# Graph attention on one core: gathers without memsets between them, and a rearranged end of each layer

## The chip, the cores and the metric

The kernel runs on one core of one Trainium2 chip. The metric is the device time of one execution in microseconds (us); the median of several executions is compared. The engines are named as in the profile: PE is TensorE's matmul, PEld its weight load, DVE is VectorE, ACT is ScalarE, POOL is GpSimd, SP is SyncE. The letter q behind a name means the engine's queue (waits, register work, issuing of transfers).

## The reference

A graph of 6250 nodes with 256 features and 200,000 edges (src, dst, 32 edge features), the edges sorted by dst. Two graph-attention layers, the first with 4 heads, the second with 1:

```python
h = relu(layernorm(x))
# per layer:
te  = relu(edge_attr @ We + be) * exp(x @ Wo + bo)[src][:, None]
hx  = (x @ Wg).reshape(n, heads, f)
al  = leaky_relu((hx*a_s).sum(-1)[src] + (hx*a_d).sum(-1)[dst] + ((te @ Wge)*a_e).sum(-1), 0.2)   # self loops added
al  = exp(al - segment_max(al, dst)[dst]);  al = al / segment_sum(al, dst)[dst]
out = segment_sum(hx[src] * al, dst) + b
# layer 0: x = relu(out + x);  layer 1: x = out + x + h;  result = input x + that
```

All arithmetic that matters here is float32.

## The kernel before

**Tables.** A prologue computes one row per node, `hx` with the node's attention terms, into a table in device memory (`T[0]`, 268 numbers a row). Layer 0 writes the rows of layer 1 into a second table (`T[1]`); each of its rows is twice 260 numbers wide, a table row and a kept input, so that layer 1 addresses it with twice the node's number.

**Steps.** The edges lie in chunks of 128, one edge per partition and chunk; a superchunk is up to 24 chunks. There are 66 superchunks to a layer: 64 of 24 chunks, then one of 14 and one of 13. `edges` walks over 132 steps, 0 to 65 for layer 0 and 66 to 131 for layer 1. A step has a dictionary `st`: its tile `G` (gathered rows), `S` (one-hot matrix by destination), `rt` and `ade` (edge and destination terms), `U` (sums by destination).

**Order.** Nothing is scheduled by a planner: the order of each engine's queue is the order in which the Python code issues (`manual_schedule`). Waits between engines are put in by the framework from the parts of tiles that instructions read and write. In `edges`, the iteration of step `st` also prepares the next step `nx`:

- POOL: `gather(nx)` issues one indirect transfer for each chunk (line 799): 128 rows, picked by a column of `self.src`, land in one chunk of `G`. Three tiles for `G` are used in turn, so the gathers of step k wait for the sums of step k-3. Behind each gather stands a memset of a tile `gap` of 208 numbers per partition (line 803); nothing reads `gap`. The rows of step 0 are gathered from `x` in the prologue (line 249), without memsets.
- DVE: `logits(st)` (lines 987 to 1002), the first to read all of `G`; `spread`, `parts`, `blocks` for `nx`; `links(st)` (1020, 1022), `maxima(st)` (1037 to 1064), `scale(st)` (1095), `carried(st)` (1077 to 1085), `edge_rows(nx)` (973, 976), `onehots(nx)` (927, 930), and `finish(pv)` for the nodes of the step before.
- PE: `ends(st)` (1010, a transpose that `links` needs), `rphase1` and `rphase2` (885, 899) and `adst` (959) for `nx`, the transpose in `links` (1027), then `sums(st)` (1105): one matmul `u += S^T G` per chunk. `rows1`, `rows2` (1198, 430) make the rows of layer 1 for finished nodes.
- ACT: the activations of `rphase1` (890), the exponentials (1060, 1135, 1147), `evict` (1110, `u` to `U`). SP: the other transfers, among them the store of a finished group of nodes in `rows3` (1239 in layer 0, 1244 in layer 1).

**A layer's end.** `ending(st, nx, pv, late, after)` replaces the loop's body where `st` is the superchunk of 14 chunks and `nx` that of 13. `pv` and `late` are earlier steps whose nodes are unfinished; `after` is the first step of the next layer, or None. In it `finish(pv, Z)` and `finish(st, Z)` do the wide part of layer 0's node update on POOL (`Z = nc.gpsimd`). `sums(nx, first=1)` takes chunk 0 last, since the sums carried over from the step before are added to that chunk. Line 750 doubles all of `self.src` at once, for layer 1's addresses. In layer 1, the nodes of the last two superchunks are stored by an indirect transfer on POOL (1249), and not on SP.

Of the kernel before, what the change touches and what calls it, by code (L numbers as in the profile page):

```python
# [22 lines left out]
F32 = mybir.dt.float32  # L23
BF = mybir.dt.bfloat16
I32 = mybir.dt.int32
AF = mybir.ActivationFunctionType
OP = mybir.AluOpType
# [4 lines left out]
P = 128  # L32
C = 24
# [46 lines left out]
class Kernel:  # L80
# [322 lines left out]
    def fixed_rows(self):  # L403
        nc, cp = self.nc, self.cp
        self.crow = cp.tile([1, D + self.L[0].H], F32, name="crow")
        self.cl = [cp.tile([36, P + 1], F32, name=f"cl{i}") for i in range(2)]
        for t in self.cl:
            nc.gpsimd.memset(t, -BIG)

        self.cnt = cp.tile([P, self.NS, 2], F32, name="cnt")  # L410
        self.mt = cp.tile([P, 4 * C + 4], F32, name="mt")
        self.gap = cp.tile([P, 208], F32, name="gap")
        self.fb = [cp.tile([P, 37 * C], F32, name=f"fb{i}") for i in range(2)]
        for t in [self.mt] + self.fb:
            nc.gpsimd.memset(t, 0.0)


        self.aq = [cp.tile([P, 4, 32], BF, name=f"aq{i}") for i in range(2)]
        for t in self.aq:
            nc.gpsimd.memset(t, 0.0)  # L420
        self.trow1 = []
        L1 = self.L[1]
        for i in range(2):
            self.trow1.append(cp.tile([P, 2 * L1.TW], F32, name=f"t1row{i}"))
            nc.gpsimd.memset(self.trow1[i][:, L1.TW + D:], 0.0)
# [135 lines left out]
    def index_group(self, g, pool, di):  # L561
# [23 lines left out]
        for pen, e in zip((self.fpen, self.lpen), ends):  # L585
            t = pool.tile([P, 4 * C], F32, name="gt", bufs=2)
            e3 = e.to_broadcast([P, n, c])
            V.tensor_sub(v3(t[:, :w]), *((d3, e3) if pen is self.fpen else (e3, d3)))
            yield
            V.tensor_scalar(pen[:, o:o + w], t[:, :w], 1.0, -BIG, op0=OP.min, op1=OP.mult)  # L590
            yield
# [117 lines left out]
    def ending(self, st, nx, pv, late, after):  # L709

        nc, k = self.nc, st["k"]
        Z = nc.gpsimd
        self.load_lb(k + 3)
        self.gather(nx)
        drain(self.logits(st))
        self.ends(st)
        self.spread(nx)
        self.parts(nx)
        y = self.rphase1(nx)
        next(y)  # L720
        self.links(st)
        if late:
            self.rows2(late)
        self.blocks(nx)
        drain(y)
        self.load_ea(k + 2)
        self.rphase2(nx)
        self.adst(nx)
        drain(self.maxima(st))
        drain(self.scale(st))  # L730
        self.carried(st)
        self.sums(st)
        self.edge_rows(nx)
        drain(self.logits(nx))
        self.ends(nx)
        self.onehots(nx)
        if late:
            self.rows3(late)
        if pv:
            drain(self.finish(pv, Z))  # L740
        self.links(nx)
        self.load_fl(k + 2)
        drain(self.maxima(nx))
        self.evict(st)
        y = self.rphase1(after) if after else iter(())
        next(y, None)
        c = nx["C"]
        drain(self.scale(nx, cuts=(1, 1 + c // 2, c)))
        if after:
            nc.vector.tensor_scalar(self.src, self.src, 2.0, None, op0=OP.mult)  # L750
        drain(self.scale(nx, cuts=(0, 1)))
        self.carried(nx)
        self.sums(nx, first=1)
        self.evict(nx)
        drain(self.finish(st, Z))
        if pv:
            self.rows1(pv)
            self.rows2(pv)
            self.rows3(pv)
        drain(y)  # L760
        f = self.finish(nx)
        while after and "hw" not in nx:
            next(f)
        self.rows1(st)
        self.rows2(st)
        drain(f)
        self.rows3(st)
        self.rows1(nx)
        self.rows2(nx)
        self.rows3(nx)  # L770
        if after:
            self.gather(after)
            self.nodes(after)
            self.spread(after)
            self.parts(after)
            self.blocks(after)
            self.rphase2(after)
            self.adst(after)
            self.edge_rows(after)
            self.onehots(after)  # L780
# [11 lines left out]
    def gather(self, st):  # L792
        nc, L = self.nc, st["L"]
        st["G"] = G = self.G0 if st["k"] == 0 else self.gp[st["k"] % 3].tile([P, C, 270], F32, name="G")
        n = self.N
        idx = self.src[:, st["o"]:st["o"] + st["C"]]
        last = st["C"] - 1
        for c in (range(0) if st["k"] == 0 and self.CX > last else (last, *range(last))):
            nc.gpsimd.indirect_dma_start(  # L799
                out=G[:, c, 0:L.TW], out_offset=None, in_=self.rows[L.l][0:n * (1 + L.l), :],  # L800
                in_offset=bass.IndirectOffsetOnAxis(ap=idx[:, c:c + 1], axis=0))
            if st["k"]:
                nc.gpsimd.memset(self.gap, 0.0)  # L803

    def pair(self, k):

# [198 lines left out]

    def ends(self, st):


        e = st["ends"]
        self.nc.tensor.transpose(self.lf[0:e.shape[1], 1:P + 1], e, self.ident)  # L1010
# [85 lines left out]
                                    .to_broadcast([P, c1 - c0, H, L.F]), op=OP.mult)  # L1096
            yield

    def sums(self, st, first=0):
        nc, L, c = self.nc, st["L"], st["C"]  # L1100
        G, S = st["G"], st["S"]
        st["u"] = self.ps_1.tile([P, 512], F32, name="u")
        for j in range(c):
            i = (j + first) % c
            nc.tensor.matmul(st["u"][:, :L.W], S[:, i, :], G[:, i, 0:L.W], start=(j == 0), stop=(j == c - 1))  # L1105

    def evict(self, st):
        L = st["L"]
# [125 lines left out]
    def rows3(self, st):  # L1234
        nc, L, s = self.nc, st["L"], st["s"]
        if L.l == 0:
            self.table_row(st)
            r = self.row(0, s)
            nc.sync.dma_start(self.T[1][ds(r, M), :], st["trow"][1:M + 1, :])
            return  # L1240
        o, out = st["o"], self.a["out"]
        if s < self.direct:
            r = self.row(1, s)
            nc.sync.dma_start(out[ds(r, M), :], o[1:M + 1, :])
        else:
            idx = self.np_.tile([P, 1], I32, name="oidx")
            nc.vector.tensor_add(idx, self.base_f[:, s:s + 1], self.iota_m)
            nc.vector.memset(idx[0:1, :], 1 << 20)
            nc.gpsimd.indirect_dma_start(  # L1249
                out=out[:, :], out_offset=bass.IndirectOffsetOnAxis(ap=idx[:, 0:1], axis=0), in_=o,  # L1250
                in_offset=None, bounds_check=self.N - 1, oob_is_err=False)
# [119 lines left out]
def drain(g):  # L1371
    for _ in g:
        pass
# [93 lines left out]
```

## Time and profile before

| | |
|---|---|
| runs | 4551.79, 4556.36, 4559.2 us (median 4556.36) |
| profiled execution | 4555.93 us, span of its instructions 4554.1 us |
| busy | PE 3065.9 us (67%), PEld 1899.5 (42%), DVE 2901.8 (64%), ACT 516.8 (11%), POOL 3915.8 (86%) |
| gathers of line 799 | 3102, 2969.6 us busy |
| memsets of line 803 | 3102, 893.3 us busy |
| granted TensorE clock | 0.743 of full speed on average |

Busy time is what an engine's instructions took. In a list of groups, behind the bar stand the busy time in us, the mean of one instruction in ns, and the idle time of the engine just before such instructions with what ended it. A timeline row is: start in us, duration in us, engine, line, operation, output <- input, count, and in brackets the engine's idle time before it and what released it. The POOL span of a gather is the work of issuing it; when its data have landed is told in a row of its own ("DMA to landing").

### The profile page before, as it was taken

To read this page: it belongs to the slowest core of one execution; us is meant where nothing else is said; L and a number is where in the kernel's file an instruction comes from. 1 tells how busy PE (TensorE), PEld (TensorE's weight loads), DVE (VectorE), ACT (ScalarE), POOL (GpSimd) and SP (SyncE) were. 2 spreads that over 40 slices of the span, in tenths; PEclk is the share of its full clock that TensorE was granted. 3 is DMA by queue.
4 is the path that set the end of the run, shared out by engine and by line. 5 is a ranking of instruction groups with operands and counts; after the bars stand their busy time and mean duration, and the time that the engine had idled before them with its cause. 6 is when DMAs were issued, how large, how long until landed. Compare 5 with 4: busy or idle time off the path is not lost. (4 is left out here: it accounts for less than half of the span.)

```text
span 4554.1 us, 37613 instructions
## 1 busy us (share of the span) xinstructions
PE 3065.9 (67%) x9916; PEld 1899.5 (42%) x9916; DVE 2901.8 (64%) x6675; ACT 516.8 (11%) x1150; POOL 3915.8 (86%) x6365
## 2 busy tenths in 40 slices
PE   8777677667677677677746566666666665666665
PEld 6444444444444344444424334333343343433433
DVE  7877667677677677676745555555554555555655
ACT  5111111111111111111100000000000000000000
POOL 6888888888888888888878888888888888888885
PEclk9877777777777777777767777777777777777777
DMA  6444444444444444444434444444444444444442
GB/s 224 130 136 134 126 129 136 124 127 136 125 128 135 125 128 135 125 130 134 119 98 124 116 128 122 118 128 128 111 128 121 124 123 128 122 116 122 128 116 74
DMA packets 231112, 576.39 MB, mean 127 GB/s; under 512 B 63097, under 2 KB 87871, under 8 KB 230825
## 3 DMA queue, kind: packets, MB, share of 16 engines
q0 software_dynamic: 150144, 422.75, 35.2%
q1 hardware_dynamic: 80331, 150.52, 10.0%
q8 instruction: 79, 1.29, 0.1%
q14 instruction: 142, 1.16, 0.1%
q10 hardware_dynamic: 416, 0.67, 0.1%
HBM read 542.72 MB, written 31.09 MB: 126 GB/s over the span
## 5 line engine op out<-in xcount | busy, mean ns | idle before, releaser
L799 POOL DMA_INDIRECT G<-T,src x3102 | 2969.6, 957 | 553.1 <-issue 518.7
L1105 PE MATMUL u<-G,S 128*128 128x270 f32 (+1 forms) x6252 | 1461.0, 393 | 106.7 <-DVE G L1085 97.6
L1105 PEld LDWEIGHTS u<-G,S 128*128 128x128 f32 x6252 | 1189.5, 192 | 388.0 <-DVE G L1085 162.1
L803 POOL MEMSET gap<- 128x208 f32 x3102 | 893.3, 288 | 1.8
L1095 DVE TENSOR_TENSOR G<-G,kps 128x6144 f32<-128x6144 f32 (+3 forms) x136 | 853.0, 6274 | 0.0
L885 PE MATMUL y<-ea,webd 64*128 64x384 f32 (+1 forms) x1056 | 749.7, 860 | 67.3 <-ACT R L890 66.7
L1010 PE MATMUL lf<-ident,fb 128*36 128x128 f32 (+1 forms) x132 | 53.3, 404 | 1093.3 <-DVE fb L1002 772.3
L987 DVE TENSOR_TENSOR G<-rt,G 128x96 f32<-128x96 f32 (+1 forms) x132 | 30.2, 228 | 1138.9 <-DMA G<-T,src 1138.6
L1010 PEld LDWEIGHTS lf<-ident,fb 128*36 128x36 f32 (+1 forms) x132 | 15.7, 119 | 1134.6 <-DVE fb L1002 819.2
L899 PE MATMUL zad<-R,wea 128*64 128x384 f32 (+1 forms) x1056 | 476.0, 815 | 0.5 <-DVE aq L952 0.3
L890 ACT ACTIVATE R<-y,webd 128x768 f32<-128x768 f32 x260 | 233.2, 897 | 2015.2 <-PE lf L1027 1647.7
L930 DVE TENSOR_TENSOR S<-kps,loc 128x3072 f32<-128x3072 f32 x132 | 437.5, 3315 | 4.5
L885 PEld LDWEIGHTS y<-ea,webd 64*128 64x128 f32 x1056 | 300.9, 314 | 311.8 <-issue 192.5
L899 PEld LDWEIGHTS zad<-R,wea 128*64 128x64 f32 x1056 | 160.7, 207 | 319.0 <-issue 214.0
L945 PE MATMUL zad<-a,Q 128*128 128x12 bf16 (+1 forms) x132 | 24.9, 188 | 174.6 <-DVE a L943 174.6
L430 PE MATMUL fin<-wg,h1T 128*128 128x260 f32 x264 | 135.3, 667 | 2.3 <-ACT h1T L1200 2.3
L973 DVE STREAM_TRANSPOSE rt<-zad 128x768 f32<-128x768 f32 (+1 forms) x130 | 124.9, 960 | 12.1 <-PE zad L959 11.2
L914 DVE TENSOR_TENSOR lb<-lb,kps 128x1536 bf16<-128x1536 bf16 (+1 forms) x68 | 112.7, 1658 | 0.0
L1110 ACT ACTIVATE U<-u 128x270 f32<-128x270 f32 (+1 forms) x132 | 51.9, 393 | 493.7 <-PE u L1105 493.7
L1041 DVE SCALAR_TENSOR_TENSOR m<-fpen,lf,m 128x24 f32<-128x24 bf16 (+1 forms) x66 | 16.4, 249 | 132.8 <-PE lf L1027 132.6
L945 PEld LDWEIGHTS <-Q 128*128 128x128 bf16 x132 | 13.7, 104 | 208.3 <-DVE a L943 198.6
L430 PEld LDWEIGHTS fin<-wg,h1T 128*128 128x128 f32 x264 | 75.6, 316 | 52.1 <-issue 36.6
(201 smaller groups left out, 2287.5 us busy)
## 6 DMA issues: line engine op xcount, KB each, us to landing
G<-T,src POOLq DMA_INDIRECT x3102, 2.8
ea<-in_ea_dram SPq DMA_DIRECT2D x64, 768.0 KB
lb<-locrow SPq DMA_DIRECT2D x64, 384.0 KB
T<-t1row SPq DMA_DIRECT2D x66, 227.5 KB
tw<-T SPq DMA_DIRECT2D x66, 225.8 KB
tw<-T SPq DMA_DIRECT2D x66, 117.2 KB
tw<-in_x_dram SPq DMA_DIRECT2D x66, 112.0 KB
out_dram<-fb SPq DMA_DIRECT2D x64, 112.0 KB
```

Of the source, the lines that this page charges most:

```text
L430: self.nc.tensor.matmul(ps[:, :L.MW], hT[:, k, :], self.wg[L.l][:, k, :], start=(k == 0), stop=(k == 1))
L799: nc.gpsimd.indirect_dma_start(out=G[:, c, 0:L.TW], out_offset=None, in_=self.rows[L.l][0:n * (1 + L.l), :], in_offset=bass.IndirectOffset ...
L803: nc.gpsimd.memset(self.gap, 0.0)
L885: nc.tensor.matmul(y[:, o], self.webd[l][r, :], ea[r, w], start=True, stop=True)
L890: nc.scalar.activation(R[:, i, :32 * c].rearrange("p (b n) -> p b n", b=2), y.rearrange("p (b n) -> p b n", b=2)[:, :, :16 * c], AF.Relu, ...
L899: nc.tensor.matmul(st["zad"][i * PH:(i + 1) * PH, o], self.wea[l][0], R[:, i, w], start=True, stop=False)
L914: V.tensor_tensor(lb[:, :, :n], lb[:, :, :n], self.k_part.unsqueeze(2).to_broadcast([P, i, n]), op=OP.is_equal)
L930: nc.vector.tensor_tensor(st["S"][:, c0:c1, :], self.k_iota.unsqueeze(1).to_broadcast(w), self.loc[:, o + c0:o + c1].unsqueeze(2).to_broad ...
L973: V.transpose(rv[:, :32 * c].rearrange("p (b n) -> p b n", b=2), z.rearrange("p (b n) -> p b n", b=2)[:, :, :16 * c])
L1010: self.nc.tensor.transpose(self.lf[0:e.shape[1], 1:P + 1], e, self.ident)
L1095: nc.vector.tensor_tensor(v, v, pw[:, c0:c1, :].unsqueeze(3) .to_broadcast([P, c1 - c0, H, L.F]), op=OP.mult)
L1105: nc.tensor.matmul(st["u"][:, :L.W], S[:, i, :], G[:, i, 0:L.W], start=(j == 0), stop=(j == c - 1))
```

## The change

1. `gather` no longer puts a memset behind each transfer, and the tile `gap` is gone.
2. `ends` doubles the step's own columns of `self.src` in layer 0; the doubling of all columns in `ending` is gone.
3. In `ending`, `sums(st)` is issued in three parts (4, 4 and 6 of 14 chunks): before `edge_rows(nx)`, behind `ends(nx)`, and behind `links(nx)`. `finish(pv)` and `finish(st)` run on DVE. `links(nx)` comes ahead of `rows3(late)` and `finish(pv)`; `evict(nx)` comes behind a part or all of `finish(st)`; the rows of finished nodes move accordingly.
4. The index of the indirect stores at the end of layer 1 is computed at the start of `ending`.

```diff
@@ fixed_rows
-        self.gap = cp.tile([P, 208], F32, name="gap")
@@ ending
-        Z = nc.gpsimd
         self.load_lb(k + 3)
         self.gather(nx)
+        for q in () if after else (st, nx):
+            q["idx"] = idx = self.np_.tile([P, 1], I32, name="oidx")
+            nc.vector.tensor_add(idx, self.base_f[:, q["s"]:q["s"] + 1], self.iota_m)
+            nc.vector.memset(idx[0:1, :], 1 << 20)
         drain(self.logits(st))
         self.ends(st)
...
         self.carried(st)
-        self.sums(st)
+        c, h = nx["C"], st["C"] // 3
+        self.sums(st, (0, h))
         self.edge_rows(nx)
         drain(self.logits(nx))
         self.ends(nx)
+        self.sums(st, (h, 2 * h))
         self.onehots(nx)
-        if late:
-            self.rows3(late)
-        if pv:
-            drain(self.finish(pv, Z))
         self.links(nx)
+        self.sums(st, (2 * h, st["C"]))
         self.load_fl(k + 2)
         drain(self.maxima(nx))
         self.evict(st)
         y = self.rphase1(after) if after else iter(())
         next(y, None)
-        c = nx["C"]
         drain(self.scale(nx, cuts=(1, 1 + c // 2, c)))
-        if after:
-            nc.vector.tensor_scalar(self.src, self.src, 2.0, None, op0=OP.mult)
         drain(self.scale(nx, cuts=(0, 1)))
         self.carried(nx)
-        self.sums(nx, first=1)
-        self.evict(nx)
-        drain(self.finish(st, Z))
+        self.sums(nx, (1, c), (0, 1))
+        if late:
+            self.rows3(late)
         if pv:
+            drain(self.finish(pv))
             self.rows1(pv)
             self.rows2(pv)
+            if not after:
+                self.rows3(pv)
+        f = self.finish(st)
+        while after and "hw" not in st:
+            next(f)
+        if not after:
+            drain(f)
+            self.rows3(st)
+        self.evict(nx)
+        drain(f)
+        if after and pv:
             self.rows3(pv)
         drain(y)
+        self.rows1(st)
+        self.rows2(st)
         f = self.finish(nx)
         while after and "hw" not in nx:
             next(f)
-        self.rows1(st)
-        self.rows2(st)
+        if after:
+            self.rows3(st)
         drain(f)
-        self.rows3(st)
         self.rows1(nx)
@@ gather
-            if st["k"]:
-                nc.gpsimd.memset(self.gap, 0.0)
@@ ends
+        if st["L"].l == 0:
+            src = self.src[:, st["o"]:st["o"] + st["C"]]
+            self.nc.vector.tensor_scalar(src, src, 2.0, None, op0=OP.mult)
@@ sums
-    def sums(self, st, first=0):
+    def sums(self, st, *parts):
...
-        st["u"] = self.ps_1.tile([P, 512], F32, name="u")
-        for j in range(c):
-            i = (j + first) % c
-            nc.tensor.matmul(st["u"][:, :L.W], S[:, i, :], G[:, i, 0:L.W], start=(j == 0), stop=(j == c - 1))
+        for a, b in parts or ((0, c),):
+            for i in range(a, b):
+                j = st["n"] = st.get("n", -1) + 1
+                if j == 0:
+                    st["u"] = self.ps_1.tile([P, 512], F32, name="u")
+                nc.tensor.matmul(st["u"][:, :L.W], S[:, i, :], G[:, i, 0:L.W], start=(j == 0), stop=(j == c - 1))
@@ rows3
-            idx = self.np_.tile([P, 1], I32, name="oidx")
-            nc.vector.tensor_add(idx, self.base_f[:, s:s + 1], self.iota_m)
-            nc.vector.memset(idx[0:1, :], 1 << 20)
+            idx = st["idx"]
             nc.gpsimd.indirect_dma_start(
```

## The prediction

> **What bounds the kernel now.** I read the page's first part (busy shares), then its fifth (costliest groups), then the waits of the two engines that could be the pace, POOL and DVE. Busy shares alone name no winner, POOL 86%, PE 67%, DVE 64%, so the waits decide.
>
> ```profile
> PE 3065.9 (67%) x9916; PEld 1899.5 (42%) x9916; DVE 2901.8 (64%) x6675; ACT 516.8 (11%) x1150; POOL 3915.8 (86%) x6365
> ...
> L799 POOL DMA_INDIRECT G<-T,src x3102 | 2969.6, 957 | 553.1 <-issue 518.7
> L803 POOL MEMSET gap<- 128x208 f32 x3102 | 893.3, 288 | 1.8
> ```
>
> The gathers and the memsets make up 3863 of POOL's 3916 us. The waits of POOL over the whole run, and those of DVE in a stretch of layer 0 (500 to 2000 us) and of layer 1 (2500 to 4300 us), in us, times, longest:
>
> ```profile
> POOL G L799 <- issue: 518.7, 3096, 2.0
> POOL G L799 <- DMA T<-t1row: 10.2, 1, 10.2
> POOL G L799 <- ACT U L1110: 5.8, 1, 5.8
> ```
> ```profile
> DVE G L987 <- DMA G<-T,src: 279.6, 45, 7.6
> ```
> ```profile
> DVE G L987 <- DMA G<-T,src: 624.9, 53, 13.0
> ```
>
> POOL waits for data once at a buffer (`ACT U`, 5.8 us) and once between the layers (10.2 us); ahead of 3096 of 3102 gathers stands only "issue", 518.7/3096 = 0.168 us each. DVE, in contrast, waits for gathered rows in every superchunk: 279.6/45 = 6.2 us in layer 0, 624.9/53 = 11.8 us in layer 1. So POOL is the pace. One period is gather + memset + issue: 0.957 + 0.288 + 0.168 = 1.413 us, 33.9 us for 24 chunks. Less its wait, DVE's cycle is 33.9 - 6.2 = 27.7 us in layer 0 and 33.9 - 11.8 = 22.1 us in layer 1: the floors if POOL gets faster. The timeline shows one period (1517.79 - 1516.38 = 1.41), and that `logits` reads 2.84 us after the last gather of its superchunk began (1520.63 - 1517.79):
>
> ```profile
> 1516.38 0.95 POOL L799 DMA_INDIRECT G<-T,src  x1 [0.16 <-issue]
> 1517.34 0.28 POOL L803 MEMSET gap<- 128x208 f32 x1
> 1517.79 0.95 POOL L799 DMA_INDIRECT G<-T,src  x1 [0.17 <-issue]
> ...
> 1520.63 0.26 DVE L987 TENSOR_TENSOR G<-rt,G 128x96 f32<-128x96 f32 x1 [4.66 <-DMA G<-T,src]
> ```
>
> **1. The memsets.** Naively the period loses 0.288 us. But this profile holds gathers without a memset behind them, those of step 0 in the prologue:
>
> ```profile
> 11.16 0.95 POOL L249 DMA_INDIRECT G<-in_x_dram,src  x1 [0.30 <-issue]
> 12.41 0.95 POOL L249 DMA_INDIRECT G<-in_x_dram,src  x1 [0.30 <-issue]
> ...
> 21.17 0.95 POOL L249 DMA_INDIRECT G<-in_x_dram,src  x1 [0.30 <-issue]
> ```
> ```profile
> L249 POOL DMA_INDIRECT G<-in_x_dram,src x24: 941/947/1187, 5.7 to 50.3; - x24
> ...
> DMA to landing us min/median/max: 2.7/5.8/6.8
> ```
> ```profile
> L799 POOL DMA_INDIRECT G<-T,src x3102: 951/952/1245, 89.3 to 4511.8; - x194
> ...
> DMA to landing us min/median/max: 2.7/2.8/8.2
> ```
>
> Between 11.16 and 21.17 stand nine starts in a row, so eight periods: (21.17 - 11.16)/8 = 1.251 us. The gap between two gathers is 0.30 us and not 0.17: a memset covers 0.13 us of something that otherwise stands open. A gather of line 799 takes 952 against 947 ns, so the quiet period becomes 1.256; today's mean is 0.008 above the quiet one (1.413 against 0.952 + 0.288 + 0.165 = 1.405, the issue as in the two brackets), and I leave those 0.008 on it: 1.264 us. The saving is 1.413 - 1.264 = 0.149, taken as 0.148 us a gather, half of the memset. The Trainium skill ("Perfetto Trace Analysis", section "DMA Instruction — SWDGE (GPSIMD)") says that a gather's shown end is when the last descriptor is written, and that the processor behind it finishes later. By that rule the 0.30 us belong to the gather and stay; the prologue's rows agree, and taking the bar at its word would give the second rival's time.
>
> Where does it count? A superchunk would take 24 x 1.264 = 30.3 us, still above DVE's 27.7 and 22.1, so POOL stays the pace. In steps 1 and 2 it buys nothing, since POOL stood 5.8 us at a buffer anyway (row above); in the last 27 chunks of a layer DVE's chain is the later one. There remain 61 full superchunks in layer 0 (steps 3 to 63) and 64 in layer 1 (66 to 129): 125 x 24 = 3000 gathers. 3000 x 0.148 = **444 us**. The bounds: 1.24 us (the prologue's period without the jitter, and a hundredth off) gives 519, 1.30 us (the jitter grown fivefold) gives 339. DVE next to a denser POOL could slow down. Its reading of `G` shows nothing of it now, at a POOL that gathers for 0.952 of 1.41 us:
>
> ```profile
> L989 DVE TENSOR_TENSOR al<-G x45: 319/321/324, 503.4 to 1995.3; 128x96 f32<-128x96 f32 x45
> ```
>
> Even 10% on all of layer 0's DVE cycle would only bring it to 30.7, 0.4 over POOL's: 61 x 0.4 = 24 us lost. That stays inside the range.
>
> **2. Doubling the sources in each step** puts 66 DVE instructions of 128x24 into layer 0 and takes one of 128x1563 out of its end.
>
> ```profile
> L750 DVE TENSOR_SCALAR src<-src x1: 965/965/965, 2286.9 to 2286.9; 128x1563 int32<-128x1563 int32 x1
> ```
> ```profile
> L927 DVE COPY kps<-lastloc x132: 148/151/154, 123.5 to 4515.9; 128x1 f32<-128x1 f32 x132
> ```
>
> One costs between 0.15 (line 927) and 0.17 us (0.151 + 0.965 x 24/1563), say 0.2: DVE's cycle becomes 27.9 us, hidden under the 30.3 by 2.4 us of waiting for gathers. Without that cover it would be 64 x 0.2 = 13 us. It writes columns that this step's gathers have read already, `logits` having waited for their landing; no gather of another step reads them, so POOL gets no wait from it. Cost taken: nothing on the path.
>
> **3. The end of layer 0.** From `logits` of the 14 chunks to the first gather of layer 1 the pace is DVE's chain and the store of the new rows, and no gather:
>
> ```profile
> 2258.59 0.22 DVE L987 TENSOR_TENSOR G<-rt,G 128x56 f32<-128x56 f32 x1 [0.20 <-DMA G<-T,src]
> ...
> 2278.00 0.61 POOL L1178 TENSOR_TENSOR fa<-tw,mw 128x256 f32<-128x256 f32 x1 [9.60 <-DVE mw L1155]
> ...
> 2279.29 0.47 DVE L1020 TENSOR_TENSOR_SCAN cl<-fl,cl,lf 4x129 f32<-4x129 f32 x1 [1.38 <-PE lf L1010]
> ...
> 2299.70 0.43 DVE L1178 TENSOR_TENSOR fa<-tw,mw 128x256 f32<-128x256 f32 x1
> ...
> 2309.75 1.06 POOL L799 DMA_INDIRECT G<-T,src  x1 [10.18 <-DMA T<-t1row]
> ```
>
> The stretch is 2309.75 - 2258.59 = 51.2 us. DVE's 1.38 us at line 1020, behind all 14 matmuls of `sums(st)`, goes with the split, as do about 1.5 us of `finish(pv)` that now come behind `links`, and 0.96 us of line 750: -4 in all. Against it the wide part of two `finish` comes from POOL (0.61 us an operation) to DVE (0.43): some six operations, 2.5 us each time. Behind `links`, DVE waits for PE's sums for part of this, so I take 3 of the 5 us. Net **-1 us**, between -4 and +5.
>
> **4. The end of layer 1.**
>
> ```profile
> 4514.86 0.18 DVE L987 TENSOR_TENSOR G<-rt,G 128x13 f32<-128x13 f32 x1 [3.06 <-DMA G<-T,src]
> ...
> 4518.70 0.27 PE L1010 MATMUL lf<-ident,fb 128*33 128x128 f32 x1
> ...
> 4520.74 0.47 DVE L1020 TENSOR_TENSOR_SCAN cl<-fl,cl,lf 1x129 f32<-1x129 f32 x1
> ...
> 4533.97 0.39 ACT L1110 ACTIVATE U<-u 128x261 f32<-128x261 f32 x1 [10.57 <-PE u L1105]
> ...
> 4539.61 1.02 POOL L1249 DMA_INDIRECT out_dram<-fb,oidx  x1 [26.59 <-DVE flagf L789]
> 4544.64 1.01 POOL L1249 DMA_INDIRECT out_dram<-fb,oidx  x1 [4.00 <-DVEq L1259]
> ```
>
> The last gather's wait of 3.06 goes: 3. Line 1020 comes 5.9 us behind `logits` (4520.74 - 4514.86), because the transpose (4518.70) is queued behind all of `sums(st)` and `finish(pv)` stands ahead of `links`; with both moved, onehots alone lies between, about 3 us: 3 saved. `finish(st)` ahead of `evict(nx)` takes a little DVE work out from behind line 1110: 1. The second indirect store now starts 4544.64 - 4539.61 = 5.03 us behind the first; if `st`'s store goes out while `nx` is still being summed, those 5 go, if not, none. I take 5, since in the new order the store stands ahead of `evict(nx)`. **-12 us**, between -4 and -16.
>
> **The sum**, against the profiled execution (span 4554.1, own time 4555.93, 0.43 below the median 4556.36): 4555.93 - 444 - 1 - 12 = 4099 us. As differences of single executions are small beside the range, I give it for the median too.
>
> **Rivals.**
>
> *Completion slots (slower).* In the built program each gather waits for the completion of the gather eight before it, as eight semaphores are used in turn. Today that wait is invisible: eight periods are 8 x 1.41 = 11.3 us, and landing takes 2.8 (8.2 at most). Back to back, transfers crowd: in the prologue landing rose from 2.8 to 5.8 us. It decides from 8 x 1.264 = 10.1 us on, and the kernel gets slower from 11.3 on. At 12 us the period is 12/8 = 1.5, 0.087 over today's: +3000 x 0.087 = 261, less 13: 4804 us. For it: landing doubled where no memset stood between. Against it: 5.8 was reached in a prologue that loads much else, and it would have to double again; a period of 1.251 was held there. The Trainium skill ("DMA: Bandwidth & Descriptors", "Anatomy of one DMA — SWDGE (gpsimd) path") gives 2.0 us plus bytes by 436 GB/s, an estimate of 2.3 us for 137 KB; the rows of line 799 (2.8) are near it, the prologue's (5.8) speak against a constant.
>
> *No hidden tail.* If the prologue's 0.30 us are its own (other tables, cold queues), the gap stays 0.168: period 0.957 + 0.168 = 1.125, 27.0 us a superchunk. Then layer 0 is DVE-bound at 27.9: 61 x 6.0 + 64 x 6.9 = 808 us, less 13: 3735 us. For it only that those are 24 gathers of one place; against it that each of them shows 0.30.
>
> *Nothing gained.* If the period is set not by POOL's instructions but by what is behind them, the gather takes the memset's time over, and only the ends remain: 4555.93 - 13 = 4543 us. Against it: the prologue's 1.251.
>
> **How the numbers follow.** The forecast has 0.83, the slots 0.08, no tail 0.05, nothing gained 0.04. A measurement can tell about 0.2% (9 us) from no change; of the last case, 13 us by my sum, 0.03 goes to faster and 0.01 to the same. Faster 0.83 + 0.05 + 0.03 = 0.91, same 0.01, slower 0.08. The forecast's own range follows from the period: 4555.93 - 519 - 13 = 4024 at 1.24, and 4555.93 - 339 - 13 = 4204 at 1.30. Since both periods are ends, I take 4030 to 4200, which holds nearly all of the 0.83 and leaves the other cases out.
>
> **What would show it.** Right: gathers of line 799 start every 1.25 to 1.27 us with 0.30 of "issue" ahead of them; DVE's wait at line 987 falls to about 30.3 - 27.9 = 2.4 us a superchunk in layer 0 and 8.2 in layer 1, and does not vanish; line 1020 stands about 3 us behind line 987 at the end; a store of line 1249 starts ahead of the last line 1110. Wrong: POOL waiting at line 799 for a semaphore of a gather, landing times above 10 us, a gather of 1.2 us and more, or "issue" back at 0.17 with DVE no longer waiting for rows.

## The result: 4082 us, and on other chips the other sign

| | before | changed | ratio (95% interval) |
|---|---|---|---|
| first measurement, 6 runs each | 4556.7 us | 4082.4 us (4080.5 to 4083.4) | 0.8962 (0.8952 to 0.8971) |
| again, chip 5 (r5_after_again) | 4554.6 | 4081.1 | 0.8961 (0.8946 to 0.8976) |
| again, chip 13 (r7_after_third) | 4756.4 | 4844.3 | 1.0184 (1.0167 to 1.0201) |

The forecast was 4099 us, 4030 to 4200. The measured 4082 lies 17 us below it. But the experiments ran on four chips. On one of them (chip 5) the times are as in the first measurement. On the three others (chips 3, 4 and 13) the kernel before is slower, and the kernels without memsets are slower still; the changed kernel itself ran there only on chip 13, the other two had near copies of it. I call them chips of the first kind (kernel before about 4555 us) and of the second (4696 to 4756 us). Each was measured at one time only, so a kind can be a chip or a state that it was in. The prediction's profile came from the first kind.

**The profile after, first kind** (span 4081.6 us, profiled execution 4083.40). The busy row of the page, and its two costliest groups, the gathers and the matmuls of `sums`; the memsets' group is gone:

```profile
PE 3035.2 (74%) x9916; PEld 1887.1 (46%) x9916; DVE 2890.5 (71%) x6752; ACT 517.3 (13%) x1152; POOL 3007.1 (74%) x3249
...
L810 POOL DMA_INDIRECT G<-T,src x3102 | 2957.2, 953 | 1018.3 <-issue 917.8
L1119 PE MATMUL u<-G,S 128*128 128x270 f32 (+1 forms) x6252 | 1463.6, 393 | 108.7 <-DVE G L1097 106.2
```

The waits of POOL over the whole run, then those of DVE from 500 to 2000 us (layer 0) and from 2200 to 3900 us (layer 1):

```profile
POOL G L810 <- issue: 917.8, 3013, 0.3
POOL G L810 <- DMA T<-t1row: 43.5, 1, 43.5
...
POOL G L810 <- ACT U L1124: 12.7, 1, 12.7
```
```profile
DVE G L996 <- DMA G<-T,src: 142.4, 49, 4.9
```
```profile
DVE G L996 <- DMA G<-T,src: 467.6, 57, 12.7
```

Issue rose from 0.168 to 917.8/3013 = 0.305 us a gather. DVE still waits for rows: 142.4/49 = 2.9 us a superchunk in layer 0 (2.4 were forecast) and 467.6/57 = 8.2 in layer 1 (8.2). POOL, now equal to PE and hardly over DVE by busy share, is still the pace, since DVE waits for its gathers, and POOL waits for data only between the layers and once at a buffer; the shares alone wouldn't tell. One period in the timeline, 1011.17 - 1009.92 = 1.25 us, and the landing times:

```profile
1009.92 0.95 POOL L810 DMA_INDIRECT G<-T,src  x1 [0.30 <-issue]
1011.17 0.95 POOL L810 DMA_INDIRECT G<-T,src  x1 [0.31 <-issue]
1012.04 0.26 DVE L996 TENSOR_TENSOR G<-rt,G 128x96 f32<-128x96 f32 x1 [1.88 <-DMA G<-T,src]
```
```profile
L810 POOL DMA_INDIRECT G<-T,src x3102: 940/946/1238, 89.6 to 4046.1; - x194
...
DMA to landing us min/median/max: 2.7/2.8/8.3
```

Where the 472.5 us between the two spans come from, by the starts of `logits` in both timelines: up to step 3, 1.3 us; steps 3 to 64, 219.9; 64 to 66 (the end of layer 0 and the first gathers of layer 1), 5.4; 66 to 129, 235.1; from step 129 to the end, 10.7. The two ends, in the timeline (the end of layer 0 runs from the first row to the second, 49.4 us where it was 51.2):

```profile
2037.35 0.22 DVE L996 TENSOR_TENSOR G<-rt,G 128x56 f32<-128x56 f32 x1 [0.21 <-DMA G<-T,src]
...
2086.72 0.94 POOL L810 DMA_INDIRECT G<-T,src  x1 [43.52 <-DMA T<-t1row]
...
4050.86 0.18 DVE L996 TENSOR_TENSOR G<-rt,G 128x13 f32<-128x13 f32 x1 [0.17 <-issue]
...
4053.47 0.27 PE L1022 MATMUL lf<-ident,fb 128*33 128x128 f32 x1
...
4053.90 0.46 DVE L1032 TENSOR_TENSOR_SCAN cl<-fl,cl,lf 1x129 f32<-1x129 f32 x1
...
4065.26 0.37 ACT L1124 ACTIVATE U<-u 128x261 f32<-128x261 f32 x1
...
4067.40 1.02 POOL L1261 DMA_INDIRECT out_dram<-fb,oidx  x1 [20.37 <-DVE mw L1141]
...
4070.57 1.00 POOL L1261 DMA_INDIRECT out_dram<-fb,oidx  x1 [2.15 <-DVE flag_i L801]
```

### The profile page after: what moved, and what is told of

It is laid out like the page before. It is cut to its first block, busy times and chain, and to the rows that moved or that the text cites. A ratio compares the mean times of both kernels' runs of the same rounds, so it can differ in the third digit from the quotient of the medians.

```text
span 4081.6 us, 34563 instructions
## 1 busy us (share of the span) xinstructions
PE 3035.2 (74%) x9916; PEld 1887.1 (46%) x9916; DVE 2890.5 (71%) x6752; ACT 517.3 (13%) x1152; POOL 3007.1 (74%) x3249
## 2 busy tenths in 40 slices
DMA packets 231089, 576.21 MB, mean 141 GB/s; under 512 B 63097, under 2 KB 87871, under 8 KB 230825
## 5 line engine op out<-in xcount | busy, mean ns | idle before, releaser
L810 POOL DMA_INDIRECT G<-T,src x3102 | 2957.2, 953 | 1018.3 <-issue 917.8
L1119 PE MATMUL u<-G,S 128*128 128x270 f32 (+1 forms) x6252 | 1463.6, 393 | 108.7 <-DVE G L1097 106.2
L894 PE MATMUL y<-ea,webd 64*128 64x384 f32 (+1 forms) x1056 | 728.0, 838 | 67.3 <-ACT R L899 66.8
L1022 PE MATMUL lf<-ident,fb 128*36 128x128 f32 (+1 forms) x132 | 49.1, 372 | 649.5 <-DVE fb L1011 500.5
L894 PEld LDWEIGHTS y<-ea,webd 64*128 64x128 f32 x1056 | 291.8, 305 | 303.3 <-issue 179.4
L1056 DVE TENSOR_TENSOR mt<-fpen,lf 128x96 f32<-128x96 bf16 (+1 forms) x66 | 16.7, 253 | 113.1 <-PE lf L1039 113.1
```

What stands on the lines that cost most here:

```text
L810: nc.gpsimd.indirect_dma_start(out=G[:, c, 0:L.TW], out_offset=None, in_=self.rows[L.l][0:n * (1 + L.l), :], in_offset=bass.IndirectOffset ...
L894: nc.tensor.matmul(y[:, o], self.webd[l][r, :], ea[r, w], start=True, stop=True)
```

## The experiments

### The memsets alone, all but the memsets, and memsets of other widths

Theory T1: behind its shown end a gather keeps POOL for 0.30 us, and a memset that fits in there is free. T2: a gather behind a memset is taken over faster (0.17 us instead of 0.30), so a tiny memset would make the period shorter than none.

`e1_no_memset`, the kernel before with

```diff
-            if st["k"]:
-                nc.gpsimd.memset(self.gap, 0.0)
```

> The kernel before without its memsets, nothing else changed. Theory (the memsets are the whole steady gain, the rearranged ends a separate 10 to 13 us): 4082 + 12 = 4094 us, 4090 to 4099; period of the gathers 1.255 us with 0.30 us of issue between them. Rival (doubling the sources or the new order also shortens the steady steps): above 4110 us, and a period over 1.26.

`e2_memset_back`, the changed kernel with these two lines and the tile of 208 columns put back:

> The changed kernel with the memset of 208 columns put back behind each gather. Theory: only the ends' gain remains, 4556.5 - 12 = 4544 us, 4541 to 4548, period 1.41 us with 0.17 us of issue. Rival (the ends gain only because gathers are faster): 4551 us and more.

`e3_memset_1` and `e4_memset_104`, the same with tiles of other widths:

```diff
+        self.gap = cp.tile([P, 1], F32, name="gap")     # e4: [P, 104]
```

> The changed kernel with a memset of 1 column (some 0.06 to 0.10 us, an estimate) behind each gather. Theory T1 (behind its shown end a gather still needs 0.30 us, and whatever POOL does in that time is free): idle and memset together stay 0.30, period 1.255 us, time 4082 us within 8. Rival T2 (a gather behind a memset is handed over in 0.17 us instead of 0.30 us, so the memset's length is simply added): period 0.953 + 0.06 to 0.10 + 0.167 = 1.18 to 1.22 us, 3000 x 0.035 to 0.075 = 105 to 225 us less, 3857 to 3977 us.

> The changed kernel with a memset of 104 columns behind each gather; by half of the 0.288 us of 208 columns, or by a fixed 0.06 and the rest in proportion, it takes 0.14 to 0.18 us (an estimate). T1: period 0.953 + the larger of 0.30 and 0.167 + 0.14 to 0.18, that is 1.26 to 1.30 us, 4097 to 4217 us. T2: the same, since both add here. A third reading (the memset's own time is hidden as long as it is under 0.30 and only then counts in full): 1.255 us, 4082 us.

All four shared one chip, of the second kind: the kernel before took 4696.1 us there. Against it, e1 took 4782.5 us (ratio 1.0188, 1.0171 to 1.0205), e2 4680.7 (0.9967, 0.9956 to 0.9978), e3 4830.0 (1.0290, 1.0273 to 1.0307), e4 4687.1 (0.9982, 0.9971 to 0.9993). None of the expected totals came true, and for e1 86 us lost stood where some 460 gained were expected. The periods, however, came out as T1 has them wherever nothing else held POOL. From e3's timeline (1.25 us from gather to gather) and e4's (1.32 us):

```profile
999.90 0.95 POOL L811 DMA_INDIRECT G<-T,src  x1 [0.19 <-issue]
1000.84 0.12 POOL L815 MEMSET gap<- 128x1 f32 x1
1001.15 0.95 POOL L811 DMA_INDIRECT G<-T,src  x1 [0.19 <-issue]
```
```profile
603.96 0.95 POOL L811 DMA_INDIRECT G<-T,src  x1 [0.17 <-issue]
604.92 0.20 POOL L815 MEMSET gap<- 128x104 f32 x1
605.28 0.95 POOL L811 DMA_INDIRECT G<-T,src  x1 [0.17 <-issue]
```

Between the end of a gather and the start of the next lie 0.30 us with no memset, 0.12 + 0.19 = 0.31 with 1 column, 0.20 + 0.17 = 0.37 with 104 and 0.288 + 0.167 = 0.455 with 208: the larger of 0.30 and the memset plus 0.17. T2 would need 0.29 for 1 column, and it was the issue that grew instead. The two differ by only 0.02 us here, but the mean over some 2950 gathers that nothing else held is 0.306 us in e3 and 0.309 in m1 (below), so T1 stands. (The memsets took 0.12 and 0.20 us, more than the 0.06 to 0.10 and the 0.14 to 0.18 that were estimated.) What the totals said was something else, which the next two runs had to place.

### The changed kernel again

> The changed kernel itself once more, because on the chip of the first four experiments the kernel before took 4696 and not 4556 us, and matmuls and vector instructions of its copies were released one by one, 0.7 or 1.4 us apart, for some 9 us in each superchunk. Theory (it is the chip, or its state at the time): where the kernel before runs at about 4556 us this runs at 4082 and no vector or matmul instruction waits over 1 us for issue; where the kernel before runs at about 4696 this runs at 4765 to 4785, slower than it, with such stalls in each step. Rival (the stalls belong to those four kernels): 4082 us on any chip.

> The kernel before without its memsets again, beside the former run. Theory (chip or state): where the kernel before takes about 4556 us, 4082 + 12 = 4094 us (4090 to 4099), the 12 being what the two layers' ends are worth in the traces; where it takes about 4696, again 4775 to 4790. Rival (the stalls belong to the kernel, not to the chip): 4780 us on any chip.

They ran on a chip of the first kind: before 4554.6, r5 4081.1 us, r6 4092.9 us (0.8989, 0.8974 to 0.9004). No such stalls appear in either trace: the matmuls of `sums` wait for issue never in r5 and once in r6 (3.1 us, as once in the kernel before). So it was the chip or its state, not the kernels, and the split of the gain is measured: 4554.6 - 4092.9 = 461.7 us for the memsets, 4092.9 - 4081.1 = 11.8 us for all the rest. e2 agrees on its chip: 4696.1 - 4680.7 = 15.4 us for the rest without the memsets' gain, with an interval of 10 to 21.

### Parts of the rearranged ends

> The changed kernel with a memset of 1 column behind each gather, as in e3_memset_1. There its gathers stood 1.25 us apart wherever nothing else held them (0.95 gather, 0.115 memset, 0.19 issue). T1 (0.30 us behind a gather are taken in any case, and a memset that fits into them is free): on a chip without the stalls 4081 us, 4076 to 4088. T2 (the memset's time is added to a shorter handover): with 0.115 + 0.167 a period of 1.235, 0.02 x 3000 = 60 us less, 4021. Third reading (any memset costs its time on top): +0.115 x 3000 = 345, 4426.

`p_sums_whole`:

```diff
-        self.sums(st, (0, h))
+        self.sums(st)
...
-        self.sums(st, (h, 2 * h))
...
-        self.sums(st, (2 * h, st["C"]))
```

> The changed kernel with all of the 14-chunk superchunk's sums issued at once, ahead of edge_rows. Theory (the split is worth the transpose's wait behind the matmuls): the transpose of line 1022 comes about 4 us later at the end of layer 1 (14 matmuls take 7.8 us from 4049.9, against 4053.5 now) and about 3 at the end of layer 0; together 3 to 8 us more than 4081.1, so 4084 to 4089. Rival (the PE is late anyway in these ends, so the order of its matmuls costs nothing): 4080.5 to 4082.

`p_finish_pool`:

```diff
-            drain(self.finish(pv))
+            drain(self.finish(pv, nc.gpsimd))
...
-        f = self.finish(st)
+        f = self.finish(st, nc.gpsimd)
```

> The changed kernel with the wide part of the two finish at the end of layer 0 on POOL again. The prediction priced the move to DVE at 3 of at most 5 us lost. By that: 3 us less than 4081.1, 4077 to 4079; DVE paces the end from 2066 to 2080 us of the trace, and two wide parts of 2.5 us go out of it. Rival (POOL's own chain of six operations of 0.61 us, twice, is later than DVE's): 0 to 3 us more, 4081 to 4084.

`p_double_end` takes the doubling out of `ends` and puts the old line back behind `next(y, None)` and the first `scale`:

> The changed kernel with all sources doubled at once at the end of layer 0, as before, and not in each step. The prediction's reading (66 small instructions hide under DVE's wait for gathered rows, which is 2.9 us a superchunk in layer 0 now): +0 to +1 us, 4081 to 4082, the wait growing to 3.1. Rival (they lie on the path): 64 x 0.2 = 13 us less, 4069.

These four met a chip of the second kind (before 4754.6 us): m1 4916.6 (ratio 1.0338, 1.0314 to 1.0362), p_sums_whole 4848.8 (1.0196), p_finish_pool 4833.7 (1.0170), p_double_end 4835.2 us (1.0169). The totals can't be held against expectations for the first kind. The ends can, for there few or no gathers run, and the same ends come near each other on both kinds. From the last `logits` to the second indirect store it is 19.71 us in the first measurement's trace, 19.71 in r5 and 19.69 in p_double_end; over all traces with this order it is 19.4 to 19.7, but 21.0 in r7 and e2. Layer 0's end, from `logits` of the 14 chunks to the first gather of layer 1, takes 48.1 to 49.4 us in the eight traces of the changed kernel and its copies with memsets. By that:

- The split of the sums. In p_sums_whole this stretch is 23.92 us, 4.2 more, and the end of layer 0 52.1 against 49.1 in p_double_end, 3.0 more. The 7 us lie within the 3 to 8 expected. In the timeline the transpose stands behind all matmuls and line 1030 7.3 us behind `logits` (3.0 in p_double_end):

```profile
4811.40 0.18 DVE L994 TENSOR_TENSOR G<-rt,G 128x13 f32<-128x13 f32 x1 [0.18 <-issue]
...
4818.41 0.27 PE L1020 MATMUL lf<-ident,fb 128*33 128x128 f32 x1
4818.72 0.47 DVE L1030 TENSOR_TENSOR_SCAN cl<-fl,cl,lf 1x129 f32<-1x129 f32 x1 [4.20 <-PE lf L1020]
```

- The wide parts of `finish`. With them on POOL, layer 0's end takes 50.5 us, 1.4 more than p_double_end's 49.1 and over all eight of 48.1 to 49.4. The rival was right that POOL is the later way; the theory had 3 us less. It is one trace, and 1.4 us is about the spread of the eight.
- The doubling. With it at the end, layer 0's end takes 49.1 us, within the values with it in each step. That the 66 instructions are hidden in the steps could not be read from a total here, but r5 and r6 show it on the first kind: a superchunk of layer 0 takes 30.04 us by the starts of `logits` in r5, with a doubling in each, and 30.05 in r6, with none. The rival's 0.2 us a superchunk isn't there.
- m1 costs 81 us against p_double_end, although POOL's quiet period is nearly the same (means of 1.262 and 1.255 us); on this kind of chip even a memset that fits in the 0.30 us isn't free. Where the 81 us go isn't shown.

### What the second kind of chip does

> The changed kernel itself a third time, beside the next run, because its copies so far ran on two kinds of chips: where the kernel before takes 4555 us and no instruction of PE or DVE is held up, and where it takes 4696 to 4755 and they are held up for some 9 us in every superchunk. Theory (the gain of 10% belongs to the first kind; on the second, denser gathers bring more of these stalls than they save): first kind 4081 us; second kind 1.5 to 2% over the kernel before, about 4770 where that takes 4696 and 4830 where it takes 4755. Rival (the slowdown there came from the edits of the experiments): 10% under the kernel before on either kind.

> The changed kernel with a memset of 104 columns behind each gather, as in e4_memset_104, where the memset took 0.198 us, the idle time behind it 0.168 and the period was 1.32 us. Theory: on a chip of the first kind 4081 + (1.32 - 1.255) x 3000 = 4276 us, 4260 to 4290; on the second kind within 0.5% of the kernel before, and faster than the changed kernel by 1.5 to 2%. Rival (a gap of 104 columns brings as many stalls as none): on the second kind as slow as the changed kernel.

The chip was of the second kind: before 4756.4, r7 4844.3 us (ratio 1.0184), r8 4714.1 us (0.9908, 0.9892 to 0.9925). The theory held for r7 (4830 expected), and the rival that the stalls belong to the edits fell with it, since r7 is the changed kernel itself. r8 did better than the theory: 0.9% under the kernel before, where within 0.5% was expected, and 2.7% under r7. So the same program has two traces. Of r7, the two costliest groups of the page, and the waits of POOL and of PE:

```profile
L810 POOL DMA_INDIRECT G<-T,src x3102 | 2955.8, 953 | 1752.2 <-issue 909.7
L1119 PE MATMUL u<-G,S 128*128 128x270 f32 (+1 forms) x6252 | 1764.3, 427 | 1222.1 <-issue 1061.9
```
```profile
POOL G L810 <- issue: 909.7, 2962, 6.9
POOL G L810 <- PE zad L954: 338.2, 62, 12.8
POOL G L810 <- PE u L1119: 249.0, 38, 8.9
POOL G L810 <- PE fin L1212: 118.2, 20, 9.2
```
```profile
PE u L1119 <- issue: 1061.9, 635, 4.5
```

Gathers take what they took, 953 ns and 0.30 us of issue. New is that the matmuls of `sums` wait for issue, 1062 us in all, 8.0 a superchunk; on the first kind all their idle time was 108.7 us, and 106.2 of it had DVE as releaser. POOL, whose next gathers need the buffer that these sums read, then waits for PE: 338 + 249 + 118 = 705 of the 753 us by which the spans differ (4834.8 - 4081.6). In the timeline of r7, from one superchunk:

```profile
1516.23 8.02 PE L1119 MATMUL u<-G,S 128*128 128x270 f32 x34 [1.14 <-DVE crow L1095]
...
1526.73 0.19 PEld L1119 LDWEIGHTS u<-G,S 128*128 128x128 f32 x1 [2.68 <-issue]
1526.81 0.43 DVE L1194 TENSOR_TENSOR fa<-fa,hw 128x256 f32<-128x256 f32 x1 [0.74 <-DVE fb L1192]
1527.20 0.94 POOL L810 DMA_INDIRECT G<-T,src  x1 [0.31 <-issue]
1527.43 0.39 PE L1119 MATMUL u<-G,S 128*128 128x270 f32 x1 [2.43 <-issue]
1528.45 0.95 POOL L810 DMA_INDIRECT G<-T,src  x1 [0.30 <-issue]
...
1529.54 0.42 DVE L1196 TENSOR_TENSOR fb<-fa,fb 128x256 f32<-128x256 f32 x1 [2.30 <-remote]
...
1530.23 0.61 PE L1119 MATMUL u<-G,S 128*128 128x270 f32 x1 [2.41 <-issue]
...
1533.74 4.60 PE L1119 MATMUL u<-G,S 128*128 128x270 f32 x10 [0.79 <-issue]
...
1538.61 0.94 POOL L810 DMA_INDIRECT G<-T,src  x1 [9.21 <-PE fin L1212]
```

Here the first 34 matmuls of `sums` run without a stall. Then PE gets a weight load or a matmul only every 0.7 or 1.4 us, and DVE one or two instructions in 1.5 to 2.7 us ("remote" is a releaser that the profile can't name), while POOL goes on at its pace. After the last gather (1528.45) the next ten matmuls run at full pace again from 1533.74 on, and POOL has to wait 9.2 us for PE. The whole trace has 128 stretches of gathers that end with a pause of over 1 us. In 125 of them PE or DVE waits over 1 us for issue or a remote releaser; the first such wait begins 21.3 us after the first gather, and the last one ends 3.0 us after the end of the last gather (medians from the timeline). So the stalls come late in a row of close gathers, and end when these pause. With 104 columns, r8's sums lose less to them:

```profile
PE u L1122 <- issue: 315.2, 240, 2.5
```

That is 2.4 us a superchunk instead of 8.0. Of the ten traces of the second kind, the seven with a period of 1.25 to 1.26 us lose 876 to 1062 us there, the two with 1.32 us 124 (e4) and 315 (r8). More pause does not end it: e2, with 1.41 us, loses 221. m1 loses 1058 us, hardly more than p_double_end (1047).

What PE and DVE wait for, and what differs in these chips, no run shows. The work is the same: r7 and the first kind's trace moved the same 231,089 packets, and DVE is busy for 2892 and 2891 us, so its instructions are held up and not slower. Two more differences are on record, and whether they are causes is open: TensorE's granted clock is 0.716 in r7 and 0.771 on the first kind, and none of the ten traces of the second kind tells when a gather's data landed, while all four of the first do.

## Why the prediction was right, and where not

**The memsets.** The step held: the prologue's rows without a memset gave the period, 1.264 us with jitter forecast. By the starts of `logits`, over 24, it fell from 1.404 to 1.252 us in layer 0 and from 1.410 to 1.255 in layer 1. The saving is thus 0.152 and 0.155 us a gather where 0.148 was taken, and 461.7 us where 444 were forecast; these 18 us, less 1 at the layers' ends, are the 17 by which the time was missed. The term that was mis-sized is the jitter: the prediction left 0.008 us of it on the new period, 3000 x 0.008 = 24 us, and it didn't carry over (the quiet 1.256 was enough). Part of that is taken back because the period before, 1.413 by the sum of means, was 0.003 to 0.009 shorter too. The Trainium skill ("Perfetto Trace Analysis", section "DMA Instruction — SWDGE (GPSIMD)") says that a gather's shown end is the writing of its last descriptor, and that the processor finishes later. This fits the 0.30 us that stay without a memset, and the 0.31 with one of 1 column; what POOL does in them no run shows.

**The doubling.** Its cover is there: 2.9 us of waiting in layer 0, where 2.4 were forecast, and r5 against r6 shows no cost.

**The end of layer 0.** -1 forecast, 49.4 - 51.2 = -1.8 measured, but with wrong parts, so that the sum came near is luck. The step that failed is "Against it the wide part of two `finish` comes from POOL to DVE ... so I take 3 of the 5 us": back on POOL they cost 1.4 us more, so the loss of 3 isn't there. The split and what goes with it were put at 4 in all; the split alone is worth 3.0. The split and the move together would give 4.4 us. The whole new end gains 1.8 in the first pair of traces, 2.7 from r6 to r5, and 4.3 to 5.2 from e1 to e2, e3 and e4, so single traces scatter too much to say whether another moved step takes some back.

**The end of layer 1.** -12 forecast, -10.7 measured. The wait for the last gathers: 18.54 to 15.97 us between the last two `logits`, 2.6 of 3 forecast. Line 1020 (now 1032) comes 3.0 us behind `logits`, as forecast, where it was 5.9. The step that failed is the store: "in the new order the store stands ahead of `evict(nx)`". It was issued 2.1 us behind it (4067.40 against 4065.26), since `finish(st)` ended only after it, and the second store follows 3.2 us behind the first where none of the 5.0 were to be left. From `evict` to the second store it is nevertheless 5.3 us instead of 10.7, close to the 5 + 1 forecast, but by another way. The prediction had overlooked in the timeline of before that the indices of both stores were computed behind both `finish`:

```profile
4539.07 0.35 DVE L1247 TENSOR_TENSOR oidx<-base,iota_m 128x1 int32<-128x1 f32 x2
```

So the first store went out 5.6 us behind `evict` there (4539.61 against 4533.97); with the indices ready from the start of `ending` it goes 2.1 us behind it. That the index does it is read from the two timelines; it was not run alone. Behind the second store 1.6 us came on top (4081.6 - 4070.57 against 4554.1 - 4544.64).

**The rivals.** "Completion slots" fell on the first kind: landing stayed at 2.8 us median, 8.3 at most (for the second kind the profile tells no landing times). "No hidden tail" fell with the 0.30, "nothing gained" with the period. The result on the second kind, 1.8% slower, is none of my rivals: I looked for the slower case in the gathers' own queue, and it came through PE, which lost its instructions' issue and then held POOL up at the buffers. The profile of before could not show it, since there the sums wait for issue once, 3.1 us.

A version for both kinds: the changed kernel with 104 columns is faster than both kernels on chip 13 (4714 against 4756 and 4844). On chip 4 it is only 0.2% under the kernel before (4687 against 4696), and the one with 208 columns (4681) is no slower. On the first its period of 1.32 us gives 4081 + 0.065 x 3000 = 4276 us, an estimate from the traces, still 6% under the kernel before and 5% over the changed one. No version tried is best on both.

## What to carry to other kernels

Before an instruction that "does nothing" is priced at its busy time, find the same neighbours without it in the same profile: here half of the memset's 288 ns was covered by what a gather needs anyway. And before it is taken out for good, run on more than one chip: what is idle time on one can, on another, be what keeps the other engines supplied.

## What the runs showed of the hardware that I had not expected

The same program came out in two kinds by chip, or by the state of a chip: 4081 and 4844 us for the changed kernel, 4555 and 4696 to 4756 for the one before. On the second kind, after some 20 us of gathers at 1.25 us each, PE and DVE fall to an instruction or two in 0.7 to 2.7 us until the gathers pause; at a period of 1.25 us PE's sums lose 876 to 1062 us to it, at 1.32 us 124 to 315, at 1.41 us 221. And POOL took 0.30 us from the end of one gather to the start of the next, which a memset of 1 column did not shorten (0.31).
